# The end of a convolution-attention kernel in written order: the recurrence takes its PSUM banks from the loop's pools

## Chip, cores and metric

One core of a Trainium2 chip runs the whole program. The metric is the device time of one execution in microseconds, and the median of several executions is quoted. All data are float32.

## What is computed

```python
# layer 0: convolution attention over 4096 positions, 4 images, 128 channels
x = x + L0_conv_ref(gn(x), ...)
# layer 1, on tokens
t = to_tokens(x)
h = ln_t(t); q = h @ W
t = t + softmax(q @ q.T) @ h
# feed-forward part: a product, batch norm over all tokens, a recurrence over tokens
Wx = ln_t(t) @ W.T
Wx = (Wx - mean) * rsqrt(var + eps) * gamma + beta
def step(yt, wx_t):
    yt = sigmoid(wx_t + yt @ V.T)
    return yt, yt
t = t + scan(step, y0 = 0, Wx)
```

`mean` and `var` run over all 4 x 4096 tokens, so no step of the recurrence can start before the last product of the feed-forward part has been seen.

## The kernel before

For each of the four images `layer0` runs one attention and `layer1` the other; blocks of 512 tokens (`QB`, numbered `n`) are the unit. `layer1` works on a symmetric score matrix: a block of it serves its own tokens directly (`direct`) and, turned, those of another block (`reversed_products`). When all parts of a block's output have been added up in `oacc`, `finish` puts three small pieces of work on the queue `pending`, from which the loop takes one at a time between its products:

- `tokens` (L652 to L659, then `layernorm`, L297 to L301): transposes to tokens, denominators, residual, statistics of the normalisation on VectorE, the inverse square root on GpSimd (L143, L144), the normalised tokens on VectorE.
- `turn` (L672, L673): transposes back, a copy to SBUF on ScalarE; its `result` turns the tokens on VectorE (L273, into the tile `d`) and sends them to DRAM (`t2_d`, L277).
- `inputs` (L681 to L685): the feed-forward product, its statistics for the batch norm (`bn_st`), and a copy into `wxs`.

In the last image the blocks 1 and 0 come last. Block 0 takes its PSUM banks for this from `ps_s`, a pool of two tiles of two banks each that the scores use otherwise; the other blocks take theirs from `ps_m` (one tile of one bank). `ps_o` has three tiles of one bank. In all eight banks.

Then comes the end of `fast`: a comparison of all denominators with bounds (`ok`, L820 to L822), the batch norm's `gain` and `bias` (L845 to L850), and the recurrence. A chain of 32 tokens is one unit, and each chain begins 12 tokens earlier from zero, so there are 44 steps (k = 0 to 43); a step handles all chains at once, split into two halves by image (`halves`). For each half a step is: a preload of the bank with `gain * wx` on VectorE (`preload`, L864), a product with `V` added onto it on TensorE (L877), and the sigmoid with `bias` on ScalarE (L881), whose result is the operand of the next product of this half. The preload for step k + 2 stands behind step k in the code. Three banks in rotation for each half make six banks, six tiles of a pool of their own (`ps_r`). Before the first preload each bank is written once with a product (L841, six of 256 columns), since the recurrence's products add onto what is there. From step 15 on VectorE also adds a finished group of outputs to the tokens, one addition per step (L891), and four stores send the result out (L896). A check of the chains' overlap (`gap`, L900 to L904) and a branch on it close the program.

The order of instructions on each engine is set by a scheduler which works with a model of costs. Exceptions are stretches under `manual_schedule`, which stand as written, and single instructions marked by `keep_in_program_order`. Waits between engines are made from the tiles that instructions read and write.

Of the kernel before, what the change touches and what calls it, by code (L numbers as in the profile page):

```python
# [10 lines left out]
F32 = mybir.dt.float32  # L11
I32 = mybir.dt.int32
AF = mybir.ActivationFunctionType
ALU = mybir.AluOpType
AX = mybir.AxisListType
PSUM = bass.MemoryType.PSUM
DRAM = bass.MemoryType.DRAM

P = 128
B, C, N = 4, 128, 4096  # L20
# [3 lines left out]
NT = N // P  # L24
EPS_GN, EPS_LN, EPS_BN = 1e-5, 1e-5, 1e-5
# [4 lines left out]
QB = 512  # L30
# [6 lines left out]
G = N // L  # L37
GB = QB // L


DEN_LO, DEN_HI = 2.0**-60, 2.0**100
# [4 lines left out]
SQ, BQ, SK, BK, SG, BG, GAMMA, BETA = range(8)  # L46
# [124 lines left out]
def fast(  # L171
# [3 lines left out]
    nc = tc.nc  # L175
    keep_ctx = ExitStack()
    keep = keep_ctx.enter_context(tc.tile_pool(name="keep", bufs=1))
    bn_st = keep.tile([P, B * NB, 6], F32, name="bn_st")
# [6 lines left out]
    with ExitStack() as st:  # L185
# [2 lines left out]
        accp = st.enter_context(tc.tile_pool(name="accp", bufs=1))  # L188
        work = st.enter_context(tc.tile_pool(name="work", bufs=1))
        stat = st.enter_context(tc.tile_pool(name="stat", bufs=4))  # L190
        ps_s = st.enter_context(tc.tile_pool(name="ps_s", bufs=2, space=PSUM))
        ps_o = st.enter_context(tc.tile_pool(name="ps_o", bufs=3, space=PSUM))
        ps_m = st.enter_context(tc.tile_pool(name="ps_m", bufs=1, space=PSUM))

# [94 lines left out]
        def layernorm(src, dst):  # L291

            mv = stat.tile([P, NQ, 2], F32, tag="mv", name="mv")
            rstd = stat.tile([P, NQ], F32, tag="rstd", name="rstd")
            for j in range(NQ):
                s6 = stat.tile([P, 6], F32, tag="s6", name="s6")
                nc.vector.bn_stats(s6, src[j])  # L297
                nc.vector.bn_aggr(mv[:, j, :], s6)  # L298
            inv_sqrt(rstd, mv[:, :, 1], EPS_LN)
            for j in range(NQ):  # L300
                nc.vector.tensor_scalar(  # L301
                    dst[j], src[j], mv[:, j, 0:1], rstd[:, j : j + 1],
                    ALU.subtract, ALU.mult,
                )
# [238 lines left out]
        def layer1(b, h, qt):  # L543
# [50 lines left out]
            def direct():  # L594
                n, a, i, e, o = fifo.popleft()
                for half in range(2):
                    nc.tensor.matmul(  # L597
                        o, lhsT=h[:, NQ * a + 2 * i + half, :], rhs=e[:, half, :],
                        start=(a == order(n)[0] and i == 0 and half == 0),
                        stop=(a == order(n)[-1] and i == 1 and half == 1),  # L600
                    )
                if a == order(n)[-1] and i == 1:
                    part(n, o)
# [24 lines left out]
            def finish(n):  # L628
                cs = bass.ts(n, QB)
                rinv = stat.tile([P, NQ], F32, tag="rinv", name="rinv")  # L630
                t = work.tile([P, 4, NQ, 32], F32, tag="t", name="t1", bufs=2)
                if b == B - 1 and n == 0:

                    one, two = (ep.tile([P, 2, QB], F32, tag="e", name="last") for _ in range(2))
                    h2, t1 = (one[:, r, :].rearrange("q (j c) -> q j c", j=NQ) for r in range(2))
                    th = two[:, 0, :]

                    def bank():
                        return ps_s.tile([P, 2, QB], F32, tag="s", name="ml")[:, 0, :]
                else:  # L640
                    h2 = work.tile([P, NQ, C], F32, tag="h2", name="h2")
                    th = work.tile([P, QB], F32, tag="th", name="th")
                    t1 = work.tile([P, NQ, C], F32, tag="og", name="t1b")

                    def bank():
                        return ps_m.tile([P, QB], F32, tag="m", name="m1")
                nc.sync.dma_start(t, t_d[b, n])

                def tokens():
                    m = bank().rearrange("q (j c) -> q j c", j=NQ)  # L650
                    for j in range(NQ):
                        nc.tensor.transpose(m[:, j, :], oacc[:, n, bass.ts(j, P)], ident)  # L652
                    at = (B + b) * NT + n * NQ
                    den = den_all[:, at : at + NQ]
                    nc.vector.tensor_reduce(den, m, AX.X, ALU.add)
                    nc.vector.tensor_scalar(den, den, 1.0 / C, None, ALU.mult)
                    nc.vector.reciprocal(rinv, den)
                    for j in range(NQ):
                        nc.vector.scalar_tensor_tensor(  # L659
                            t1[:, j, :].rearrange("q (p i) -> q p i", p=4),  # L660
                            m[:, j, :].rearrange("q (p i) -> q p i", p=4), rinv[:, j : j + 1],
                            t[:, :, j, :], ALU.mult, ALU.add,
                        )
                    layernorm(quarters(t1), quarters(h2))

                def result():
                    turn_out(t1.rearrange("q j (p i) -> q j p i", p=4), t2_d[b, :, cs])

                def turn():
                    m = bank()  # L670
                    for j in range(NQ):
                        nc.tensor.transpose(m[:, bass.ts(j, P)], h2[:, j, :], ident)  # L672
                    nc.scalar.copy(  # L673
                        th.rearrange("c (p j k) -> c j p k", j=NQ, p=4),
                        m.rearrange("c (j p k) -> c j p k", j=NQ, p=4),
                    )
                    result()

                def inputs():
                    m = bank()  # L680
                    nc.tensor.matmul(m, lhsT=wt["f"], rhs=th, start=True, stop=True)  # L681
                    nc.vector.bn_stats(bn_st[:, b * NB + n, :], m)
                    m = m.rearrange("p (g i s) -> p i g s", i=L // 2, s=2)
                    if b == B - 1:
                        nc.vector.tensor_copy(wxs[:, :, b, bass.ts(n, GB), :], m)  # L685
                    else:
                        wx = work.tile([P, L // 2, GB, 2], F32, tag="wx", name="wx")
                        nc.vector.tensor_copy(wx, m)
                        nc.sync.dma_start(wxs_d[b, :, :, bass.ts(n, GB), :], wx)

                if b == B - 1 and n == 0:
                    pending.appendleft(tokens)
                    pending.extend([turn, inputs])
                elif b == B - 1 and n < 4:
                    pending.extend([tokens, turn, inputs])
                else:
                    pending.extend([tokens, nothing, nothing, nothing, turn, inputs])


            for n in [NB - 2, NB - 1] + list(range(NB - 3, -1, -1)):  # L700
                o = None
# [53 lines left out]
                        turned.append((clock + 4, n, a, t))  # L755
            while fifo:
                direct()
            pending.extend([reversed_products] * len(turned))

        def own_bank(_):  # L760
            return ps_m.tile([P, 512], F32, tag="m", name="mp")
# [53 lines left out]
        flush()  # L815


        tc.keep_in_program_order(nc.scalar.activation(first_y, shift, AF.Sigmoid))
        ok = big.tile([P, 2, 2 * B * NT], F32, tag="oacc", name="ok")
        nc.vector.tensor_scalar(ok[:, 0, :], den_all, DEN_LO, None, ALU.is_ge)  # L820
        nc.vector.tensor_scalar(ok[:, 1, :], den_all, DEN_HI, None, ALU.is_le)
        nc.vector.tensor_reduce(par_ok[:, 1:2], ok.rearrange("p a b -> p (a b)"), AX.X, ALU.min)  # L822


    with ExitStack() as st:
        scan = st.enter_context(tc.tile_pool(name="scan", bufs=1))
        ps_r = st.enter_context(tc.tile_pool(name="ps_r", bufs=1, space=PSUM))
        t2 = scan.tile([P, B, N], F32, name="t2s")
        for b in range(B):
            nc.sync.dma_start(t2[:, b, :], t2_d[b])  # L830
        y = scan.tile([P, L // 2, B, G, 2], F32, name="y")
        state = scan.tile([P, B, G + 1], F32, name="state")
        nc.gpsimd.memset(state[:, :, 0:1], 0.0)

        HB = B // 2
        banks = [[ps_r.tile([P, 512], F32, tag=f"r{s}{i}", name="ps_r") for i in range(3)] for s in range(2)]
        for s in range(2):
            for i in range(3):  # L840
                nc.tensor.matmul(  # L841
                    banks[s][i][:, : HB * G], lhsT=ident, rhs=wxs[:, 0, :HB, :, 0],
                    start=True, stop=True, skip_group_check=True,
                )
        nc.vector.bn_aggr(mv, bn_st.rearrange("p a b -> p (a b)"))  # L845
        inv_sqrt(gain, mv[:, 1:2], EPS_BN)
        nc.vector.tensor_mul(gain, gain, col(GAMMA))

        nc.vector.tensor_mul(bias, mv[:, 0:1], gain)
        nc.vector.tensor_sub(bias, col(BETA), bias)  # L850

        halves = [slice(s * HB, (s + 1) * HB) for s in range(2)]
        steps = list(range(L - W, L)) + list(range(L))

# [14 lines left out]
        for k, i in enumerate(steps):  # L869
# [15 lines left out]
            if k >= W:  # L885
                todo.extend((i - 3, b) for b in range(B) if i % 4 == 3)
                for j in range(len(todo) if i == L - 1 else min(1, len(todo))):
# [7 lines left out]
                    if i0 == L - 4:  # L895
                        nc.sync.dma_start(out[b], t2[:, b, :])  # L896


        gap = scan.tile([P, B, G - 1], F32, name="gap")
        nc.vector.tensor_sub(gap, state[:, :, 1:G], at(y, L - 1, slice(0, B))[:, :, : G - 1])  # L900
# [406 lines left out]
```

## Time and profile before

| | us |
|---|---|
| median of 3 runs | 3049.04 (3047.84 to 3049.8) |
| profiled execution | 3049.66 |
| its span, first to last instruction | 3047.8 |
| mean granted TensorE clock | 0.993 |
| TensorE busy (matmul) | 2990.5 |
| VectorE busy | 1678.8 |
| ScalarE busy | 1033.2 |
| GpSimd busy | 219.4 |

The page of the profile lists the busy times, a strip of 40 slices, the chain of work that ended last, and the costliest groups of instructions. Times in the timeline are counted from the start of the span. An instruction of TensorE shows as passes: a float32 product has two, each with a weight load (PEld) and a matmul (PE).

The last product of the attention loop ends near 2944 us. What follows, up to the end of the span, is the stretch that the change touches: from 2944 to 2963 the last two blocks and the batch norm, from 2963 to 3020.7 the recurrence, then the stores.

### The profile page before, as it was taken

How to read it: one execution, taken by the hardware profiler on the slowest of the kernel's cores; microseconds unless marked ns; L12 is line 12 of the kernel's file. 1: busy time of each engine (PE TensorE's matmuls, PEld its weight loads, DVE VectorE, ACT ScalarE, POOL GpSimd, SP SyncE). 2: the span in 40 equal slices, each digit the busy share in tenths (PEclk: the TensorE clock that was granted, in tenths of full speed). 3: DMA queues.
4: the chain of work that ended last, by engine and by line, in shares of the span. 5: the costliest groups of instructions: out<-in, count | busy, mean ns of one | idle time of the engine just before them, and what ended most of it. 6: DMA issues, size and time to landing. Idle time of an engine off the chain costs nothing.

```text
span 3047.8 us, 31523 instructions
## 1 busy us (share of the span) xinstructions
PE 2990.5 (98%) x10720; PEld 1370.7 (45%) x10720; DVE 1678.8 (55%) x3113; ACT 1033.2 (34%) x1150; POOL 219.4 (7%) x215
## 2 busy tenths in 40 slices
PE   8999999999999999999999999999999999999985
PEld 4444444444444444444444444444444444444442
DVE  6666654434666664443466665443456666333356
ACT  3444432222344432222244443222234443222224
POOL 0111100000011110000011011000001111000000
PEclk9999999999999999999999999999999999999998
DMA  1111143434111123343312114343422112544333
GB/s 42 39 55 56 51 115 87 96 88 101 44 56 56 44 86 97 91 101 85 89 46 56 39 49 117 85 99 88 99 59 56 42 49 88 145 100 101 97 117 153
DMA packets 247562, 241.09 MB, mean 79 GB/s; under 512 B 90080, under 2 KB 162272, under 8 KB 246368
## 3 DMA queue, kind: packets, MB, share of 16 engines
q1 hardware_dynamic: 247392, 238.98, 29.4%
q8 instruction: 88, 1.44, 0.2%
q14 instruction: 82, 0.67, 0.1%
HBM read 65.80 MB, written 56.62 MB: 40 GB/s over the span
## 4 chain that ended last, share of the span: by engine, by line
PE 93%; DVE 3%; SPq 2%; ACT 1%; DMA 0%; issue 0%; POOL 0%; DVEq 0%; ACTq 0%; POOLq 0%
PE o L468 28%; PE o L597 15%; PE ps L236 14%; PE ps L718 14%; PE ot L610 12%; SPq L752 2%; PE m L265 1%; PE m L681 1%; PE mp L430 1%; PE ps L570 1%; PE mp L366 1%; PE mq L562 1%; PE mp L415 1%; DVE t2s L891 1%; DVE ps_r L864 1%; PE m L672 1%
## 5 line engine op out<-in xcount | busy, mean ns | idle before, releaser
L468 PE MATMUL o<-e,nxt 64*128 64x512 f32 x4096 | 973.1, 589 | 0.0
L238 ACT ACTIVATE e<-ps 128x1024 f32<-128x1024 f32 x512 | 521.6, 1025 | 687.1 <-PE ps L236 649.7
L245 DVE TENSOR_TENSOR acc<-acc,e 128x1024 f32<-128x1024 f32 x448 | 547.7, 1223 | 230.7 <-ACT e L238 214.0
L468 PEld LDWEIGHTS o<-e,nxt 64*128 64x128 f32 x4096 | 403.3, 187 | 483.0 <-issue 474.2
L236 PE MATMUL ps<-nxt 64*128 64x512 f32 x2048 | 541.6, 595 | 1.3 <-ACT e L584 0.8
L597 PE MATMUL o<-e,h 128*128 128x512 f32 x1160 | 537.0, 592 | 0.0
L722 ACT ACTIVATE e<-ps,shift 128x1024 f32<-128x1024 f32 x258 | 287.4, 1114 | 646.3 <-PE ps L718 360.4
L718 PE MATMUL ps<-qt 128*128 128x512 f32 x1032 | 482.9, 594 | 2.7 <-ACT qt L563 2.7
L610 PE MATMUL ot<-tt,h 128*128 128x512 f32 x888 | 400.9, 593 | 0.0
L725 DVE STREAM_TRANSPOSE dd<-e 128x512 f32<-128x512 f32 x444 | 281.7, 683 | 137.1 <-ACT e L722 91.9
L597 PEld LDWEIGHTS o<-e,h 128*128 128x128 f32 x1160 | 218.8, 190 | 268.2 <-issue 268.0
L236 PEld LDWEIGHTS ps<-nxt 64*128 64x128 f32 x2048 | 197.9, 187 | 230.3 <-issue 148.6
L718 PEld LDWEIGHTS ps<-qt 128*128 128x128 f32 x1032 | 189.9, 190 | 219.3 <-issue 189.6
L610 PEld LDWEIGHTS ot<-tt,h 128*128 128x128 f32 x888 | 167.8, 190 | 210.2 <-issue 204.9
L619 DVE TENSOR_TENSOR oacc<-oacc,ot 128x512 f32<-128x512 f32 x87 | 59.8, 687 | 288.2 <-PE ot L610 288.2
L143 POOL TENSOR_SCALAR rstd<-mv 128x4 f32<-128x4 f32 x64 | 14.6, 228 | 2371.6 <-DVE mv L298 2371.6
L524 DVE SCALAR_TENSOR_TENSOR t<-yt,rinv,t 128x128 f32<-128x128 f32 x128 | 36.5, 347 | 78.1 <-DMA yt<-turn_d 78.1
L485 POOL TENSOR_SCALAR xb<-xb,bpc 128x512 f32<-128x512 f32 x32 | 59.7, 1866 | 250.6 <-DMA xb<-in_x_dram 244.9
L535 POOL TENSOR_SCALAR h<-h 128x512 f32<-128x512 f32 x32 | 72.4, 2262 | 63.8 <-DVE d L273 61.7
L580 ACT ACTIVATE e<-ps,shift 128x512 f32<-128x512 f32 x32 | 22.0, 687 | 143.5 <-PE ps L576 118.5
L144 POOL TENSOR_TENSOR rstd<-rstd,mhalf 128x4 f32<-128x4 f32 x64 | 66.4, 1038 | 5.3
L621 DVE COPY oacc<-ot 128x512 f32<-128x512 f32 x24 | 16.6, 692 | 87.2 <-PE ot L610 87.1
(156 smaller groups left out, 1613.5 us busy)
## 6 DMA issues: line engine op xcount, KB each, us to landing
tt<-dd SPq DMA_DIRECT2D x1776, 64.0 KB, 2.0
turn_d<-d SPq DMA_DIRECT2D x384, 64.0 KB, 1.8
xb<-in_x_dram SPq DMA_DIRECT2D x32, 256.0 KB, 3.3
t<-turn_d SPq DMA_DIRECT2D x32, 256.0 KB, 2.7
yt<-turn_d SPq DMA_DIRECT2D x32, 256.0 KB, 2.7
t_d<-t SPq DMA_DIRECT2D x32, 256.0 KB, 2.0
qt<-turn_d SPq DMA_DIRECT2D x32, 256.0 KB, 2.8
t<-t_d SPq DMA_DIRECT2D x32, 256.0 KB, 2.9
```

Of the source, the lines that this page charges most:

```text
L144: nc.gpsimd.tensor_tensor(dst, dst, mhalf[:, :n], ALU.pow)
L236: nc.tensor.matmul(ps[:, h, :], lhsT=lhsT, rhs=rhs, start=True, stop=True)
L238: nc.scalar.activation(e, ps, AF.Exp, scale=scale)
L245: nc.vector.tensor_tensor(acc, acc, e, ALU.add)
L468: nc.tensor.matmul(o[r], lhsT=v[rs, p + h * PAIRS, :], rhs=e[rs, h, :], start=(p == 0 and h == 0), stop=(p == PAIRS - 1 and h == 1),)
L535: nc.gpsimd.tensor_scalar(hn, hn, 1.0, None, ALU.add)
L597: nc.tensor.matmul(o, lhsT=h[:, NQ * a + 2 * i + half, :], rhs=e[:, half, :], start=(a == order(n)[0] and i == 0 and half == 0), stop=(a = ...
L610: nc.tensor.matmul(ot, lhsT=h[:, NQ * n + j, :], rhs=t[:, :, j, :, :].rearrange("q p k j -> q k p j"), start=(j == 0), stop=(j == NQ - 1),)
L718: nc.tensor.matmul(ps[:, half, :], lhsT=qt[:, bass.ts(at, P)], rhs=qt[:, bass.ts(n, QB)], start=True, stop=True,)
L722: nc.scalar.activation(e, ps, AF.Exp, bias=shift)
L725: nc.vector.transpose(d.rearrange("q f b k j -> q k b f j")[:, 2 * i + half], e[:, half, :].rearrange("q (b f j) -> q b f j", b=NQ, f=NQ),)
L752: nc.sync.dma_start(t[bass.ts(f, 32), p], d[bass.ts(p, 32), f])
```

## The change

It does five things.

1. The three PSUM pools live until the end of `fast`, and the recurrence's six banks come from them. The function `take_banks`, called in `tokens` of the last image's block 0 behind its transposes, takes both tiles of `ps_s` (each tile gives one bank for half 0 and one for half 1), one tile of `ps_o` and the tile of `ps_m`. It marks the six banks with products of 256 columns from `oacc` and adds four products of 512 columns into one of them. The pool `ps_r` and the marks at L841 are gone.
2. Block 0 of the last image takes its banks from `ps_o` instead of `ps_s`.
3. From behind the last loop product of the last image everything stands as written (`manual_schedule`).
4. In this stretch the order is another: `bn_aggr` and the gain come ahead of the copy of block 0 into `wxs`; the comparison of the denominators stands behind the recurrence; block 1's `tokens` come with `nothing` behind them.
5. `layernorm` writes each aggregate one statistic later.

```diff
-        ps_s = st.enter_context(tc.tile_pool(name="ps_s", bufs=2, space=PSUM))
-        ps_o = st.enter_context(tc.tile_pool(name="ps_o", bufs=3, space=PSUM))
-        ps_m = st.enter_context(tc.tile_pool(name="ps_m", bufs=1, space=PSUM))
+        ps_s = keep_ctx.enter_context(tc.tile_pool(name="ps_s", bufs=2, space=PSUM))
+        ps_o = keep_ctx.enter_context(tc.tile_pool(name="ps_o", bufs=3, space=PSUM))
+        ps_m = keep_ctx.enter_context(tc.tile_pool(name="ps_m", bufs=1, space=PSUM))
...
+            sums: deque = deque()
             for j in range(NQ):
                 s6 = stat.tile([P, 6], F32, tag="s6", name="s6")
                 nc.vector.bn_stats(s6, src[j])
-                nc.vector.bn_aggr(mv[:, j, :], s6)
+                sums.append((mv[:, j, :], s6))
+                if j > 0:
+                    nc.vector.bn_aggr(*sums.popleft())
+            nc.vector.bn_aggr(*sums.popleft())
...
                     def bank():
-                        return ps_s.tile([P, 2, QB], F32, tag="s", name="ml")[:, 0, :]
+                        return ps_o.tile([P, QB], F32, tag="o", name="ml")
...
                         nc.tensor.transpose(m[:, j, :], oacc[:, n, bass.ts(j, P)], ident)
+                    if b == B - 1 and n == 0:
+                        take_banks(oacc[:, 1, :])
...
-                    if b == B - 1:
+                    if b == B - 1 and n == 0:
+                        last_inputs.append(m)
+                    elif b == B - 1:
                         nc.vector.tensor_copy(wxs[:, :, b, bass.ts(n, GB), :], m)
...
+                elif b == B - 1 and n == 1:
+                    pending.extend([tokens, nothing, turn, inputs])
...
             while fifo:
                 direct()
+            if b == B - 1:
+
+                keep_ctx.enter_context(tc.manual_schedule())
             pending.extend([reversed_products] * len(turned))
+        HB = B // 2
+        banks = [[None] * 3 for _ in range(2)]
+        last_inputs = []
+
+        def take_banks(some):
+            def mark(m, cols):
+                nc.tensor.matmul(
+                    m[:, :cols], lhsT=ident, rhs=some[:, :cols], start=True, stop=True,
+                    skip_group_check=True,
+                )
+
+            for i in (1, 2):
+                pair = ps_s.tile([P, 2, QB], F32, tag="s", name="ps_r")
+                for r in range(2):
+                    banks[r][i] = pair[:, r, :]
+            banks[0][0] = ps_o.tile([P, QB], F32, tag="o", name="ps_r")
+            banks[1][0] = ps_m.tile([P, QB], F32, tag="m", name="ps_r")
+            for r in range(2):
+                for i in range(3):
+                    mark(banks[r][i], HB * G)
+            for _ in range(4):
+                mark(banks[0][0], QB)
...
-        tc.keep_in_program_order(nc.scalar.activation(first_y, shift, AF.Sigmoid))
-        ok = big.tile([P, 2, 2 * B * NT], F32, tag="oacc", name="ok")
-        nc.vector.tensor_scalar(ok[:, 0, :], den_all, DEN_LO, None, ALU.is_ge)
-        nc.vector.tensor_scalar(ok[:, 1, :], den_all, DEN_HI, None, ALU.is_le)
-        nc.vector.tensor_reduce(par_ok[:, 1:2], ok.rearrange("p a b -> p (a b)"), AX.X, ALU.min)
+        nc.scalar.activation(first_y, shift, AF.Sigmoid)
+        nc.vector.bn_aggr(mv, bn_st.rearrange("p a b -> p (a b)"))
+        inv_sqrt(gain, mv[:, 1:2], EPS_BN)
+        nc.vector.tensor_copy(wxs[:, :, B - 1, :GB, :], last_inputs[0])
+        nc.vector.tensor_mul(gain, gain, col(GAMMA))
...
-        ps_r = st.enter_context(tc.tile_pool(name="ps_r", bufs=1, space=PSUM))
...
-        banks = [[ps_r.tile([P, 512], F32, tag=f"r{s}{i}", name="ps_r") for i in range(3)] for s in range(2)]
-        for s in range(2):
-            for i in range(3):
-                nc.tensor.matmul(
-                    banks[s][i][:, : HB * G], lhsT=ident, rhs=wxs[:, 0, :HB, :, 0],
-                    start=True, stop=True, skip_group_check=True,
-                )
-        nc.vector.bn_aggr(mv, bn_st.rearrange("p a b -> p (a b)"))
-        inv_sqrt(gain, mv[:, 1:2], EPS_BN)
-        nc.vector.tensor_mul(gain, gain, col(GAMMA))
...
+        ok = scan.tile([P, 2, 2 * B * NT], F32, name="ok")
+        nc.vector.tensor_scalar(ok[:, 0, :], den_all, DEN_LO, None, ALU.is_ge)
+        nc.vector.tensor_scalar(ok[:, 1, :], den_all, DEN_HI, None, ALU.is_le)
+        nc.vector.tensor_reduce(par_ok[:, 1:2], ok.rearrange("p a b -> p (a b)"), AX.X, ALU.min)
```

## The prediction

> **What bounds the kernel now.** The change touches only what follows the last loop product, so I read the chain of waits over the last 150 us first, then the timeline there, then the table of stretches with the granted clock. The page's chain gives PE 93%: up to 2944 us the loops are TensorE's own work, and nothing there is edited. From 2944 on the chain hops between engines. Columns: start us, us, what.
>
> ```profile
> 2949.29 0.59 DVE wxs L685
> 2951.13 0.60 DVE d L273
> 2952.19 1.05 POOL rstd L144
> 2953.66 1.26 PE ml L672 x4
> 2954.95 0.59 ACT last L673
> 2955.59 2.09 PE ml L681 x2
> 2957.70 0.70 DVE bn_st L682
> 2958.40 0.60 DVE wxs L685
> 2959.13 4.82 PE ps_r L841 x12
> ...
> 2965.73 0.49 ACT y L881
> 2966.27 0.73 PE ps_r L877 x2
> 2967.03 0.50 ACT y L881
> 2967.57 0.73 PE ps_r L877 x2
> ...
> 3017.86 0.59 DVE t2s L891
> 3018.45 0.79 DVE ps_r L864 x2
> 3019.23 3.60 DVE t2s L891 x6
> ```
>
> Three things to see. The six bank marks (L841) stand on the chain for 4.82 us. In the recurrence one half costs 0.76 us from the start of its product to the start of its sigmoid (2966.27 to 2967.03) and 0.54 us from there to its next product: 1.30 us a step. Near the end VectorE sets the pace: 0.79 for two preloads and 0.59 for one addition, 1.38 us. How two halves fit into 1.30 us shows the timeline (start, us, engine, line, what; in brackets the idle time before):
>
> ```profile
> 2966.27 0.30 PEld L877 LDWEIGHTS ps_r<-y,w 128*128 128x128 f32 x2 [0.53 <-ACT y L881]
> 2966.74 0.30 PEld L877 LDWEIGHTS ps_r<-y,w 128*128 128x128 f32 x2 [0.18 <-ACT y L881]
> 2967.03 0.97 ACT L881 ACTIVATE y<-ps_r,bias 128x256 f32<-128x256 f32 x2 [0.34 <-PE ps_r L877]
> ```
>
> The second half's product starts at 2966.74, 0.29 us before the first half's sigmoid of the same step. The halves overlap by half a step. The clock (stretch, length, busy time of PE, PEld, DVE, ACT, POOL, then PEclk):
>
> ```profile
> 2944.00:2948.60 4.60, 2.74 (x11) 1.22 (x10) 3.71 (x13) 0.59 (x1) 1.08 (x2) 1.00 0.23 57
> 2948.60:2953.60 5.00, 0.00 (x0) 0.00 (x0) 4.39 (x16) 0.00 (x0) 1.27 (x2) 0.58 0.11 28
> 2953.60:2956.00 2.40, 1.66 (x5) 1.14 (x6) 0.78 (x4) 1.03 (x2) 0.00 (x0) 0.50 0.20 51
> 2961.00:2963.50 2.50, 2.50 (x8) 2.00 (x7) 2.01 (x7) 1.12 (x2) 0.00 (x0) 0.58 0.98 419
> 2963.50:2966.00 2.50, 2.38 (x10) 1.29 (x9) 1.90 (x4) 1.22 (x3) 0.00 (x0) 1.00 1.00 423
> ```
>
> The clock falls to half at about 2949.5, after TensorE thinned out, and returns at about 2963.1 under the marks, just before the recurrence.
>
> **What the skill says.** "TensorE: Matmul & The Clock Gate", Part 1: half clock after an idle window of 3413 ns, full after a busy one, in free-running windows. The trace agrees: 2949.5 to 2963.1 is 13.6 us, four windows. "PSUM — Partial Sum Buffer", on bank collisions: engines have to be kept apart by bank, and different banks may be used at once. The recurrence before agrees: six banks in six tiles, and TensorE writes one while ScalarE reads another.
>
> **Part 1: the banks.** Before, six tiles of one bank. After, steps k with k mod 3 = 1 or 2 take both halves' banks from one two-bank tile of ps_s; only k mod 3 = 0 has separate tiles (ps_o, ps_m). Waits are made per tile, not per bank. In the changed program's instruction list the second half's product of such a step waits for the first half's sigmoid of the same step, where before it waited for its own half's sigmoid of the step before. The hardware doesn't need that wait, but it is executed.
>
> Step by step, from first-half product h0 and second-half product h1: in a pair step h1 starts 1.30 after h0 (0.76 + 0.54). The next step's h0 needs no further wait and follows h1 at once; its sigmoid follows h1's by 0.45 us (two sigmoids in 0.94 us at 3012.84, where products already run back to back). So h1 to next h1 is 0.76 + 0.45 + 0.54 = 1.75 us. Into k mod 3 = 0, h1 waits for its own half: 1.30. From there h0 of the next step starts at 1.75 and its h1 at 1.75 + 1.30 = 3.05. Three steps: 3.05 + 1.75 = 4.80 us, 1.60 a step against 1.30 to 1.37 now. VectorE fits below that: per three steps two preload pairs that now wait for each other (0.49 + 0.06 + 0.39, about 0.95 each), one of 0.79 and three additions of 0.59 make 4.46 us; so the additions no longer set the pace.
>
> Products run for k = 1 to 43. From the first to the second h1: 3.05; 13 rounds of 4.80: 62.4; the last two steps to the end of the last sigmoid: 3.05 + 0.76 + 0.49 = 4.30. Sum 69.75 us. Before: from 2963.56 to 3020.66, 57.1. **Loss 12.65 us.**
>
> **Part 2: from 2944 to the first product.** The instruction list shows what moves; one end for each:
> - L820 goes behind the recurrence, and the fourth L659 comes ahead of L682. The two early marks beside the L672 transposes (256 columns at 0.43 us each: L570 has 0.86 for four passes, and a product has two) and one between those transposes delay the n = 1 product by some 0.2 us: L682 at 2948.8 instead of 2948.6, statistics of n = 0 at 2950.0 (before 2950.06).
> - The transpose into d (L273, 0.60) leaves the gap ahead of the last aggregate: rstd is done about 0.6 us sooner, h2 ready at 2953.75 instead of 2954.4.
> - The other three marks and the four extra products stand on TensorE ahead of the h2 transposes. The first of them waits for the n = 1 copy (its bank), 2950.0. At full clock 3 x 0.43 + 4 x 0.86 = 4.7 us: to 2954.75, 1.0 us past h2. Then four transposes 0.6 us (1.26 at half clock before), copy 0.59, product 1.15 to the statistics (2.1 before): L682 at 2957.2 instead of 2957.70. At half clock they would last to 2959.4; I take full, since the early marks raise TensorE's work in the window before 2949.5.
> - The aggregate goes ahead of the wxs copy, which then lies beside GpSimd: gain ready at 2960.0 instead of 2960.93, bias at 2960.55 instead of 2961.76. L841 is gone from behind it.
> - The first product waits for both preloads of its tile, 2960.5 + 0.49 + 0.06 + 0.49 + 0.05: 2961.6 instead of 2963.56. **Gain 1.9 us.**
> - Moved DMAs: the four t2_d stores now leave SP after h2, near 2954.5; with 1.77 us to issue four and 1.8 to land they end near 2958, before the sigmoid that waits for them at 2960.6. The t2s loads still follow the n = 0 product. The memset stands behind the gain on GpSimd and nobody waits for it before step 12. All nothing.
>
> **Part 3: the clock at the start of the recurrence.** TensorE is now idle from 2957.0 to 2961.6, 4.6 us, longer than a window: the clock falls to half before the recurrence. There a product costs 0.43 more and a step about 2.3 us. Until one busy window has passed (1.7 to 6.8 us, half a window taken plus one, 5.1) each us loses 1 - 1.6/2.3 = 0.3: **loss 1.5 us**, bounds 0 and, if the clock never returns, 43 x 0.7 = 30.
>
> **Part 4: the end.** VectorE is no longer behind: the first output store leaves 0.5 us before the last sigmoid ends, not 0.39 after it. The stores still take 22 us. **Gain 0.9 us.** The ok operations (0.26 + 0.26 + 0.69) lie beside these stores, as the gap check (done at 3026) does: nothing. The new order of aggregates in layernorm leaves VectorE's order in the loops as it was: nothing.
>
> **Sum:** 12.65 - 1.9 + 1.5 - 0.9 = +11.35 us. The profiled execution took 3049.66 for a span of 3047.8; the median of the runs is 3049.04, 0.6 less. So 3061.0 for that execution and 3060.4 for a median.
>
> **Rivals.**
> - A, as worked out: 3057 to 3064. Chance 0.62.
> - B, the clock drops again and again. Products fill 6 x 0.43 of 4.80 us, 54%. A window of 55% (7.2 to 10.6 us, the tail of the warming products) kept full clock, one of 35% (2946.1 to 2949.5) lost it; two pair steps alone fill 49%. Each drop costs 1 to 2 us: 3064 to 3077. Chance 0.18.
> - C, it never returns. At half clock the products fill 5.16 of 6.9 us, 75%; the window to 2959.7 with some 51% did not lift it, the full one to 2963.1 did. 3077 to 3091. Chance 0.1.
> - D, the chained halves cost less than half of what I work out, since another overlap makes up for it: 3050 to 3056. Chance 0.06.
> - E, faster: the front of the recurrence alone decides, without marks, ok work and transpose. That is right if the halves still overlap: then -1.9 - 0.9 = 3046.2. It decides as soon as a step stays under 1.36 us on average (57.1 / 43 = 1.33 now, and parts 2 to 4 leave 1.3 over 43 steps). For it speaks that the banks are as distinct as before, against it the wait in the program. Chance 0.04.
>
> The forecast is that of A, 3060.4. The range 3056 to 3077 holds A and B. A measurement of this kernel can tell about 0.2% (6 us) from no change: slower 0.93, same 0.04, faster 0.03.
>
> **What would show it.** In the changed trace: second-half weights loading 0.54 us after the first half's sigmoid begins, not before it; sigmoids in a rhythm of 1.75, 1.75, 1.30 us; VectorE with idle time in the recurrence; the first recurrence product near 2961.6; half clock there for one or two windows; the L783 products up to 2954.8. Wrong would be a step of 1.3 us in the recurrence, half clock in its middle, or a first product after 2964.

## The result, and the profile after

| | before | after |
|---|---|---|
| median, 6 runs each (us) | 3047.96 (3047.32 to 3049.80) | 3060.57 (3058.69 to 3061.04) |
| profiled execution | 3049.66 | 3060.72 |
| its span | 3047.8 | 3059.0 |
| front: last addition into `oacc` to first product of the recurrence | 19.46 | 17.58 |
| recurrence: first product to end of last sigmoid | 57.1 | 72.95 |
| behind the last sigmoid | 27.2 | 25.6 |

The ratio is 1.004, with a 95% interval of 1.0029 to 1.0051: the changed kernel is 12.6 us slower. The lower three rows split this difference. The front starts with VectorE's last addition into `oacc` (at 2944.10 before, at 2942.90 after). The span grew by 11.2 us. The front gives -1.9, the recurrence +15.85, the end -1.6, and what lies ahead of the front -1.2: the profiled run of before began with one more window of half clock, at 17 to 21 us, in code that the change does not touch. (Of the eleven profiled executions here, the four with such an extra window near their start have that addition at 2943.97 to 2944.21, the other seven at 2942.54 to 2942.97.)

The chain of waits of the changed kernel (start us, us, what) runs through the front into the recurrence:

```profile
2948.90 5.00 PE ps_r L783 x14
2953.89 0.45 PE ml L678 x4
...
2955.00 1.14 PE ml L687 x2
2956.17 0.71 DVE bn_st L688
...
2959.48 0.41 DVE ps_r L888
2959.92 0.50 DVE ps_r L888
...
2960.51 1.21 PE ps_r L901 x2
...
2964.93 3.89 PE ps_r L901 x8
```

The marks (L783) are still on the chain and take 5.00 us against 4.82 before, but they now stand ahead of the last feed-forward product and run at full clock. Behind them the four transposes take 0.45 us and the product 1.14, against 1.26 and 2.09. (For the transposes the clock is not the main reason, as experiment 5 shows.) Two preloads (L888) stand one behind the other ahead of the first product, as the wait on the pair tile demands. Eight passes in 3.89 us are 0.49 each; the clock is at half there, as the stretches further down show.

ScalarE's timeline in the recurrence of the changed kernel (start, us, engine, line, what; in brackets the idle time before), where the clock is full again:

```profile
2970.13 0.94 ACT L905 ACTIVATE y<-ps_r,bias 128x256 f32<-128x256 f32 x2 [0.81 <-PE ps_r L901]
2971.89 0.94 ACT L905 ACTIVATE y<-ps_r,bias 128x256 f32<-128x256 f32 x2 [0.81 <-PE ps_r L901]
2973.18 0.94 ACT L905 ACTIVATE y<-ps_r,bias 128x256 f32<-128x256 f32 x2 [0.35 <-PE ps_r L901]
```

Each line is two sigmoids: that of the second half of one step and, right behind it, that of the first half of the next. The starts are 1.76 and 1.29 us apart; the next, at 2974.93 in the chain, is 1.75 further. The long distances show 0.81 us of idle ScalarE, the short one 0.35.

TensorE's side, some steps later (the same kind of view):

```profile
2985.49 0.75 PEld L901 LDWEIGHTS ps_r<-y,w 128*128 128x128 f32 x4 [1.00 <-ACT y L905]
2986.78 0.30 PEld L901 LDWEIGHTS ps_r<-y,w 128*128 128x128 f32 x2 [0.55 <-ACT y L905]
2987.24 0.30 PEld L901 LDWEIGHTS ps_r<-y,w 128*128 128x128 f32 x2 [0.15 <-ACT y L905]
2988.53 0.75 PEld L901 LDWEIGHTS ps_r<-y,w 128*128 128x128 f32 x4 [1.00 <-ACT y L905]
```

A line with four weight loads is one second-half product and the first-half product of the next step, back to back, behind 1.00 us without a load. The cause of that idle time is ScalarE's y. The load at 2988.53 comes right behind the second of the two sigmoids that run from 2987.55 to 2988.49; its own operand is the result of the first, so it has waited for the sigmoid of the *other* half. Where a step has separate tiles, its second half (2986.78) loads after a gap of 0.55, and the first half of the next step 0.46 us behind it (2987.24), each behind its own sigmoid.

The stretches of the changed kernel around the start of the recurrence, cut where the granted clock changes (stretch, length, busy time of PE, PEld, DVE, ACT, POOL, then PEclk and DMA):

```profile
2955.57:2958.98 3.41, 0.56 (x2) 0.00 (x0) 2.31 (x4) 0.88 (x2) 0.86 (x3) 1.00 0.55 131
2958.98:2962.39 3.41, 1.31 (x3) 0.62 (x3) 2.96 (x9) 1.61 (x3) 0.00 (x0) 0.50 0.95 408
2962.39:2965.81 3.42, 2.84 (x6) 1.84 (x7) 0.97 (x2) 0.97 (x2) 0.00 (x0) 0.50 1.03 441
2965.81:2969.22 3.41, 2.99 (x7) 1.38 (x6) 1.84 (x4) 1.84 (x4) 0.00 (x0) 0.50 1.01 432
2969.22:2972.63 3.41, 2.55 (x9) 1.55 (x10) 1.20 (x3) 1.79 (x5) 0.00 (x0) 1.00 0.99 423
```

After a window with 0.56 us of products the clock was at half for three windows, from 2958.98 to 2969.22. The middle one of the three, with TensorE busy for 2.84 of 3.42 us, did not bring the full clock back; the last one, with 2.99, did.

### The profile page after: what moved, and what is told of

It reads as the page before. It is cut to its first block, busy times and chain, and to the rows that moved or that the text cites. A ratio compares the mean times of both kernels' runs of the same rounds, so it can differ in the third digit from the quotient of the medians.

```text
span 3059.0 us, 31491 instructions
## 1 busy us (share of the span) xinstructions
PE 2991.4 (98%) x10728; PEld 1372.9 (45%) x10728; DVE 1680.7 (55%) x3113; ACT 1031.5 (34%) x1150; POOL 218.5 (7%) x215
## 4 chain that ended last, share of the span: by engine, by line
PE 93%; DVE 2%; SPq 2%; ACT 2%; issue 0%; DMA 0%; POOL 0%; DVEq 0%; POOLq 0%
PE o L472 28%; PE o L601 15%; PE ps L236 14%; PE ps L728 14%; PE ot L614 12%; SPq L762 2%; PE ps_r L901 1%; PE m L265 1%; ACT y L905 1%; PE m L687 1%; PE mp L434 1%; PE ps L574 1%; PE mq L566 1%; PE mp L370 1%; PE mp L419 1%; PE m L678 1%
## 5 line engine op out<-in xcount | busy, mean ns | idle before, releaser
L901 PE MATMUL ps_r<-y,w 128*128 128x256 f32 x168 | 52.8, 437 | 22.9 <-ACT y L905 16.4
L144 POOL TENSOR_TENSOR rstd<-rstd,mhalf 128x4 f32<-128x4 f32 x64 | 66.4, 1037 | 5.3
```

Source lines behind the costliest of these rows:

```text
L144: nc.gpsimd.tensor_tensor(dst, dst, mhalf[:, :n], ALU.pow)
L901: nc.tensor.matmul(bank(k, s), lhsT=wt["vt"], rhs=before, start=False, stop=True, skip_group_check=True,)
```

## The experiments

Two theories stood at the outset. The *tile theory*: the wait that the pair tile makes between the two halves costs some 13 us in the recurrence. The *clock theory*: the new front, with its marks, its extra products and its gap, lets the clock fall, and the recurrence is slow for that. They differ in what a kernel does that has the new front without pairs, or the pairs without the new front.

**1. The changed kernel, six separate tiles (`r1_split`).** The pools are the same; two tiles of `ps_s` give one bank each, and the last tile of `ps_o` is taken once block 0 has been copied out of it.

```diff
             for i in (1, 2):
-                pair = ps_s.tile([P, 2, QB], F32, tag="s", name="ps_r")
-                for r in range(2):
-                    banks[r][i] = pair[:, r, :]
-            banks[0][0] = ps_o.tile([P, QB], F32, tag="o", name="ps_r")
-            banks[1][0] = ps_m.tile([P, QB], F32, tag="m", name="ps_r")
-            for r in range(2):
-                for i in range(3):
-                    mark(banks[r][i], HB * G)
+                banks[0][i] = ps_s.tile([P, 2, QB], F32, tag="s", name="ps_r")[:, 0, :]
+                banks[1][i] = ps_o.tile([P, QB], F32, tag="o", name="ps_r")
+            banks[0][0] = ps_m.tile([P, QB], F32, tag="m", name="ps_r")
+            for r, i in ((0, 1), (1, 1), (0, 2), (1, 2), (0, 0)):
+                mark(banks[r][i], HB * G)
...
+        banks[1][0] = ps_o.tile([P, QB], F32, tag="o", name="ps_r")
+        nc.tensor.matmul(
+            banks[1][0][:, : HB * G], lhsT=ident, rhs=bc.rearrange("p a b -> p (a b)")[:, : HB * G],
+            start=True, stop=True, skip_group_check=True,
+        )
```

> The changed kernel with six separate tiles for the six banks (one bank each of the two ps_s tiles, two of ps_o, ps_m, and the last one taken from ps_o behind the copy of block 0); marks and the four extra products stay. Theory of the tile's wait: the halves overlap again, a step takes 1.30 us at full clock and 1.73 at half, the recurrence from first product to last sigmoid 57 to 60 us instead of 72.95; the whole 3046 to 3049. Rival, the half clock at the start and the written order are the cost: the rhythm of 1.75, 1.75, 1.30 stays, the recurrence takes over 68 us, the whole 3058 to 3061.

Measured: 3046.39 us (3045.41 to 3047.04), against 3047.91 for the kernel before on the same chip; ratio 0.9994 (0.9985 to 1.0003). The recurrence went from 72.95 to 58.2 us. The timeline of this kernel's recurrence:

```profile
2972.51 0.30 PEld L903 LDWEIGHTS ps_r<-y,w 128*128 128x128 f32 x2 [0.25 <-ACT y L907]
2972.73 1.03 ACT L907 ACTIVATE y<-ps_r,bias 128x256 f32<-128x256 f32 x2 [0.27 <-PE ps_r L903]
2973.26 0.30 PEld L903 LDWEIGHTS ps_r<-y,w 128*128 128x128 f32 x2 [0.45 <-ACT y L907]
2973.81 0.30 PEld L903 LDWEIGHTS ps_r<-y,w 128*128 128x128 f32 x2 [0.25 <-ACT y L907]
2974.02 0.48 ACT L907 ACTIVATE y<-ps_r,bias 128x256 f32<-128x256 f32 x1 [0.26 <-PE ps_r L903]
```

The weights at 2972.51 are those of the first half's product. They load 0.22 us before the second half's sigmoid of the step before starts (2972.73). The second half's own weights follow at 2973.26, when that sigmoid has ended; the first half's sigmoid of their step only begins then (2973.27). No half waits for the other any more, and the next pair of sigmoids follows after 1.29 us. Besides the tiles only the order of the six marks changed, and the place and source of one of them. With nearly the same front, and with half clock at the start of the recurrence here too (until 2964.71), the slow recurrence is gone, which the clock theory does not allow. The whole is not clearly different from the kernel before.

**2. Pairs along the other axis (`r2_by_half`).** One line: a tile of `ps_s` now holds two steps' banks of *one* half, so that the halves are free of each other again, and a half is tied to itself.

```diff
                 for r in range(2):
-                    banks[r][i] = pair[:, r, :]
+                    banks[i - 1][r + 1] = pair[:, r, :]
```

> The changed kernel with the two-bank tiles dealt out the other way: each ps_s tile holds two steps' banks of one half. Theory of the tile's wait: the products of the two halves no longer wait for each other, only preloads and products of neighbouring steps of one half do; two steps of 1.30 and one of 1.4 at first, and of up to 2.0 once VectorE's additions stand between; the recurrence 62 to 66 us, the whole 3050 to 3055. Rival, two banks next to each other cost as such, whichever waits there are: the recurrence stays at 70 to 73 us, the whole at 3058 to 3062.

Measured: 3053.25 us (3051.61 to 3055.0), ratio 1.0016 (1.0009 to 1.0023); recurrence about 64 us. Its ScalarE timeline:

```profile
2986.87 0.94 ACT L905 ACTIVATE y<-ps_r,bias 128x256 f32<-128x256 f32 x2 [0.36 <-PE ps_r L901]
2988.90 0.94 ACT L905 ACTIVATE y<-ps_r,bias 128x256 f32<-128x256 f32 x2 [1.09 <-PE ps_r L901]
2990.20 0.94 ACT L905 ACTIVATE y<-ps_r,bias 128x256 f32<-128x256 f32 x2 [0.36 <-PE ps_r L901]
2991.49 0.94 ACT L905 ACTIVATE y<-ps_r,bias 128x256 f32<-128x256 f32 x2 [0.36 <-PE ps_r L901]
```

Now two steps of three take 1.30 us and one 2.03. Earlier in this recurrence, before VectorE's additions begin (2983.70), the long step takes 1.42. What is late is in the view of waits of this kernel from 2980 on (who waits for whom: us in total, times, longest):

```profile
PE ps_r L901 <- DVE ps_r L888: 7.3, 9, 0.9
```

TensorE waits for VectorE's preloads, nine times. It fits that the preloads of two steps now share a tile, so that the earlier step's product also waits for the later step's preload, at a time when VectorE has its additions to do; which wait it is was not followed further. 57.1 + 7.3 = 64.4 lies near the 64 us, but the sum is rough: this recurrence also has half clock until 2966.2. How much a pair costs depends on which two users share it, not only on there being one.

**3. The kernel before, with pairs alone (`r3_before_pairs`).** The counterpart: nothing of the change but the shape of the tiles, in the old pool `ps_r`.

```diff
-        banks = [[ps_r.tile([P, 512], F32, tag=f"r{s}{i}", name="ps_r") for i in range(3)] for s in range(2)]
+        pairs = [ps_r.tile([P, 2, 512], F32, tag=f"p{i}", name="ps_r") for i in range(2)]
+        alone = [ps_r.tile([P, 512], F32, tag=f"r{s}", name="ps_r") for s in range(2)]
+        banks = [[alone[s], pairs[0][:, s, :], pairs[1][:, s, :]] for s in range(2)]
```

> The kernel before with nothing changed but the tiles of the recurrence's banks: steps with k mod 3 = 1 and 2 have both halves in one two-bank tile. The marks stay ahead of the recurrence, so the clock is full there. Theory of the tile's wait: the rhythm of 1.75, 1.75, 1.30 us, the recurrence 69.5 to 70.5 us instead of 57.1, the end about 1 us closer behind it, the whole 11 to 12.5 us above the kernel before, 3059 to 3061. Rival, it takes the pools of the loop or the written order: no change, 3047 to 3049.

Measured: 3069.54 us in the median of four runs, ratio 1.0071 (1.0054 to 1.0088), and the four runs fall apart: 3061.04, 3067.66, 3071.42 and 3071.59. The first is the profiled one; its mean clock is 0.995, that of the others 0.989 to 0.991. Its recurrence takes 70.1 us at full clock, and its ScalarE timeline has the rhythm of the changed kernel (1.75, 1.30, 1.75):

```profile
2989.09 0.94 ACT L883 ACTIVATE y<-ps_r,bias 128x256 f32<-128x256 f32 x2 [0.81 <-PE ps_r L879]
2990.84 0.94 ACT L883 ACTIVATE y<-ps_r,bias 128x256 f32<-128x256 f32 x2 [0.81 <-PE ps_r L879]
2992.14 0.95 ACT L883 ACTIVATE y<-ps_r,bias 128x256 f32<-128x256 f32 x2 [0.35 <-PE ps_r L879]
2993.89 0.94 ACT L883 ACTIVATE y<-ps_r,bias 128x256 f32<-128x256 f32 x2 [0.81 <-PE ps_r L879]
```

So the tiles alone, without any of the new front, bring 13 us: 70.1 against 57.1. The median is outside of what was expected, by 8.5 us, and the mean clock says where to look. That needed a profile of one of the long runs.

**4. The same kernel, three more executions (`r7_pairs_again`, `r8_pairs_third`, `r9_pairs_fourth`).**

> The kernel before with tiles of two banks once more, for a trace of a run of about 3070 us: three of its four runs took 3067.7 to 3071.6 at a mean clock of 0.989 to 0.991, one 3061.0 at 0.995. If the clock falls inside the recurrence, the table of stretches shows half clock there for several windows and steps of about 2.6 us, and the recurrence lasts some 80 us; if the profile is again of a run of about 3061, steps stay at 1.75, 1.75, 1.30 and it lasts 70 us.

> The kernel before with tiles of two banks, a third time, for the trace of a run above 3066 us. If the clock falls inside the recurrence: half clock there, steps of about 2.6 us, the recurrence over 75 us. Otherwise 70 us and 3061.

> The same kernel a fourth time, with the same two outcomes: above 3066 us with half clock inside the recurrence, or 3061 with full clock.

Measured: 3061.9, 3061.51 and 3070.89 us; the clocks 0.994, 0.994 and 0.990. The third is one of the long ones. First the stretches of the short run `r7_pairs_again`, then those of the long run `r9_pairs_fourth`, again window by window:

```profile
2957.88:2961.30 3.42, 3.30 (x8) 2.69 (x9) 1.69 (x5) 0.52 (x2) 0.81 (x2) 0.50 0.78 316
2961.30:2964.71 3.41, 1.89 (x8) 0.96 (x6) 2.17 (x5) 1.07 (x3) 0.00 (x0) 1.00 1.04 440
2964.71:2968.13 3.42, 2.64 (x9) 1.64 (x10) 1.29 (x3) 1.79 (x5) 0.00 (x0) 1.00 0.97 417
```

```profile
2960.95:2964.36 3.41, 3.41 (x9) 2.65 (x9) 1.22 (x5) 1.12 (x2) 0.81 (x2) 0.50 0.97 413
2964.36:2967.77 3.41, 1.82 (x7) 0.94 (x7) 1.77 (x5) 0.49 (x1) 0.00 (x0) 1.00 1.02 430
2967.77:2971.18 3.41, 2.83 (x8) 1.64 (x6) 0.97 (x2) 1.25 (x3) 0.00 (x0) 0.50 0.99 423
...
2984.84:2988.25 3.41, 2.88 (x7) 1.33 (x5) 1.85 (x4) 1.95 (x4) 0.00 (x0) 0.50 0.00 0
2988.25:2991.66 3.41, 2.67 (x10) 1.65 (x10) 1.34 (x3) 1.80 (x4) 0.00 (x0) 1.00 0.00 0
```

Both get the full clock back under the marks. The first window at full clock holds the tail of the marks, a gap, and the first products. In the short run TensorE is busy for 1.89 of its 3.41 us (55%), and the clock stays; in the long run for 1.82 (53%), and it falls. Then the paced recurrence keeps TensorE busy for 2.83 or 2.84 of each window, which did not lift the clock five times in a row; it took six windows until one with 2.88 did. At half clock three steps take 7.10 us (sigmoids at 2971.76, 2978.86 and 2985.95), against 4.80. Over 20.5 us that is 20.5 x (1 - 4.80 / 7.10) = 6.6 us. The recurrence also starts 2.6 us later (2966.1 against 2963.5), 1.2 of them from ahead of block 1's inverse square root (L144 at 2944.18 and 2943.00) and 1.4 from the front, where this run was at half clock sooner. 6.6 + 2.6 = 9.2, against 9.0 for the two spans (3069.2 and 3060.2). The other three long runs were not profiled. Their clocks are like this one's; that they have the same cause is likely and not shown.

**5. Without the extra products (`r4_no_extra`).** The changed kernel less these two lines:

```diff
-            for _ in range(4):
-                mark(banks[0][0], QB)
```

> The changed kernel without the four extra products of 512 columns; the six marks stay. Theory: the transposes of the last block start when its tokens are ready, 1.1 us sooner; if the clock holds, the whole is 1.1 us shorter; if it falls in the gap, the transposes take 0.6 and the product 0.9 us longer and nothing is won: 3059.0 to 3061.0, the recurrence unchanged at 71 to 73.5. Rival, the extra products are what holds TensorE up and costs the time: 4 us shorter, 3056.5.

Measured: 3059.42 us, ratio 1.0042 (1.0025 to 1.0059); four runs, three within 3059.33 to 3059.49 and one of 3065.31 with a clock of 0.991, not profiled. The chain of waits of this kernel, by the side of that of the changed kernel shown above:

```profile
2951.14 0.36 DVE last L305
...
2951.54 1.11 PE ml L678 x4
...
2953.32 1.33 PE ml L687 x2
2954.67 0.71 DVE bn_st L688
...
2959.01 1.21 PE ps_r L899 x2
```

Its stretches, cut where the granted clock could change (every 3.41 us):

```profile
2947.30:2950.71 3.41, 1.56 (x6) 1.06 (x6) 2.37 (x10) 0.00 (x0) 0.87 (x2) 1.00 0.00 0
2950.71:2954.12 3.41, 1.90 (x6) 0.85 (x6) 1.73 (x5) 1.42 (x2) 0.40 (x1) 1.00 0.09 21
2954.12:2957.53 3.41, 0.51 (x1) 0.00 (x0) 2.36 (x4) 0.65 (x2) 0.86 (x3) 0.50 0.46 106
```

The four transposes take 1.11 us here and 0.45 in the changed kernel, but that is not the clock, which is full until 2954.12. Each transpose needs its own quarter of the normalised tokens, and VectorE (L305) finishes one about every 0.26 us from 2951.14 on; in the changed kernel the extra products hold the transposes back until all quarters are there, and they run in one go. (`r6_all` below has the same 1.11 us, at full clock throughout.) The clock falls only inside the product, which takes 1.33 us instead of 1.14. So the extra products do hold the clock, but that is worth only 0.19 us ahead of the statistics. Against it they stand in front of the transposes. Counted from the inverse square root of block 1 (L144, at 2942.63 here and 2942.92 there), the transposes end 1.4 us sooner without them, and the first product of the recurrence comes 1.2 us sooner. What they buy is less than what they cost, by 1.2 us.

**6. Products in the gap (`r5_fill`).** The changed kernel with four products of 512 columns behind the last feed-forward product, where TensorE has nothing to do while VectorE and GpSimd work out gain and bias:

```diff
+        for _ in range(4):
+            nc.tensor.matmul(
+                banks[0][0], lhsT=ident, rhs=bc.rearrange("p a b -> p (a b)"),
+                start=True, stop=True, skip_group_check=True,
+            )
```

> The changed kernel with four more products of 512 columns (from the constant bc, into a bank that is still free) behind the last feed-forward product, where TensorE was idle for 4.4 us; nothing else. Theory: the clock is full when the recurrence starts, its first two steps take 1.75 instead of 2.65, it lasts 70 to 70.5 us instead of 72.95, the whole 2.5 to 3 us shorter, 3057.5 to 3058.5, with single runs up to 10 us longer where the clock falls inside the recurrence, as in the kernel before with tiles of two banks. Rival, the time lost at the start is the longer way to the first product and not the clock: no change, 3060 to 3061.

Measured: 3058.71 us (3058.2 to 3060.03), ratio 1.0033 (1.002 to 1.0047). Its stretches:

```profile
2957.00:2961.50 4.50, 3.63 (x9) 1.33 (x7) 3.65 (x9) 1.31 (x4) 0.87 (x3) 1.00 0.68 215
2961.50:2965.00 3.50, 2.26 (x8) 1.33 (x9) 2.47 (x6) 1.78 (x4) 0.00 (x0) 1.00 1.02 435
```

The clock is full throughout. The recurrence takes 70.2 us, 2.8 less than in the changed kernel: the price of half clock at its start. The four products delay nothing: from the end of the last feed-forward product to the first product of the recurrence it is 4.38 us here (2957.20 to 2961.58) and in the changed kernel (2956.13 to 2960.51).

**7. All together (`r6_all`).** Six tiles as in 1, the four products as in 6, and two extra products in place of four.

```diff
-            for _ in range(4):
+            for _ in range(2):
                 mark(banks[0][0], QB)
```

> Six separate tiles, two extra products instead of four ahead of the last block's transposes, and four behind the last feed-forward product. Theory: first product of the recurrence 1 us sooner than in the changed kernel, full clock there, steps of 1.30 us, the recurrence 56.5 to 57.5 us; the whole 3043.5 to 3045.5, about 3 us under the kernel before and 2 us under six tiles alone. Rival, the front doesn't get shorter because the products stand in the way: 3046 to 3048.

Measured: 3043.92 us (3042.55 to 3045.61, 21 runs), against 3049.02 (26 runs) for the kernel before on the same chip; ratio 0.9984 (0.9978 to 0.9991). It is faster than both kernels. Its chain of waits:

```profile
2951.73 1.11 PE ml L678 x4
...
2953.50 1.14 PE ml L687 x2
...
2958.82 0.73 PE ps_r L907 x2
2959.58 0.49 ACT y L911
2960.07 0.04 issue
2960.12 0.73 PE ps_r L907 x2
2960.87 0.49 ACT y L911
```

The first product of the recurrence takes 0.73 us, not 1.21, and from there a step takes 1.30. From the oacc addition to that product it is 16.04 us (before: 19.46), and the recurrence takes 56.7 (before: 57.1).

## Why the prediction was right

The forecast was 3060.4 us, slower; the median is 3060.57. That the totals agree within 0.2 us is in part luck: the forecast stood on a median before of 3049.04, and that of the six runs is 3047.96, so the change forecast was +11.35 us and the change measured is +12.6. By its own steps:

- **Part 1, the banks (12.65 us):** right, in mechanism and in size. The rhythm of 1.75, 1.75 and 1.30 us is in the trace to 0.01 us. At full clock throughout, the recurrence took 70.1 to 70.2 us (`r3_before_pairs`, `r5_fill`), where 69.75 was worked out. Taking only the pairs away removed 14.75 us (`r1_split`), of which a part is clock, since half clock ended sooner there. With the pairs and without at full clock it is 70.2 against 56.7 (`r5_fill`, `r6_all`), and adding only the pairs to the kernel before brought 13 (`r3_before_pairs`).
- **A small thing in part 1 was off.** That VectorE "fits below" is right for most of the recurrence; the last four rounds of three steps took 4.91 to 4.92 us instead of 4.80, 0.48 us in all, while VectorE was busy for 92% of the time. Whether VectorE is the cause was not tried.
- **Part 2, the front (gain 1.9):** right, 1.88. The marks ended at 2953.9, the last statistics began at 2956.17, the first product at 2960.5; each is 0.8 to 1.1 us ahead of the forecast time, which is the 1.2 us that this run was ahead from the beginning, less 0.1 to 0.4. One reading in it was wrong without harm to the sum: the 1.26 us of the four transposes before were put down to half clock, but at full clock they took 1.11 (`r4_no_extra`, `r6_all`), at the pace of VectorE's quarters. They are short in the changed kernel only because the extra products make them late, which cost the path 1.2 us.
- **Part 3, the clock (loss 1.5):** right in mechanism, too small. The term was 5.1 us at half clock; it was 8.7 us of the recurrence, since the window with 2.84 us of products did not count as a busy one. Twice two steps took 4.42 and 4.45 us (from the first product at 2960.51 to a product at 2964.93, and from there to 2969.38) for what takes 3.05 at full clock: 2.8 us lost, and 2.8 by the difference to `r5_fill`. The "half a window taken plus one" should have been two windows and a half.
- **Part 4, the end (gain 0.9):** right. The first store leaves 0.54 us ahead of the last sigmoid's end (3032.89 and 3033.43), where it was 0.39 behind. From the first store to the end of the span it took another 0.7 less (26.1 against 26.8), which was not foreseen.

The terms add up: 12.65 + 2.8 + 0.48 is 15.9, against 15.85 for the recurrence. The total for the profiled execution (3061.0 forecast, 3060.72 measured) came out nearly exact in part because the 1.3 us missing in part 3 and the 0.5 in part 1 were made good by 0.7 at the end and by the 1.2 us ahead of the front, which were not in the sum.

Of the rivals, B (the clock falls inside the recurrence) did not show in the times of the six runs of the changed kernel, of which one was profiled. It is no idle one: the kernel before with the same pairs fell into it in the one long run that was profiled. C (it never returns) had the right observation, that the paced recurrence does not lift the clock, but in that run it came back after six windows. D and E are out: the wait is real and nothing makes up for it. The shares that the prediction gives under B and C for three windows of the kernel before (55, 35 and 51%) are not the busy shares of the profile, which has 60% (2.04 of 3.41 us), 51% (1.72 of 3.40) and 57% (1.95 of 3.42). So its 54% for the paced recurrence can't be set beside the busy times quoted here.

On the Trainium skill: "PSUM — Partial Sum Buffer" has it, on bank collisions, that engines have to be kept apart by bank. `r1_split` shows that nothing more is needed in this recurrence, since with a tile for each bank ScalarE reads one while TensorE writes another, at 1.29 us a step. "TensorE: Matmul & The Clock Gate", Part 1, has the clock come back after one busy window of some 3.4 us. The lengths agree (in the traces here every stretch at half clock within the work is a multiple of 3.41 us); what counts as busy is stricter than a TensorE that is seldom idle, as 2.84 of 3.42 us did not do.

## What to carry to other kernels

Waits follow the tile, so two banks in one tile tie everything that uses them: give each of two chains that are to overlap its own tile, and when tiles are re-used from another pool, look at who shares them with whom before counting what the pool saved. In a chain of small products, read the wait of a late instruction and ask whether it is for its own operand or only for its neighbour's. Products that keep the clock belong into TensorE's idle time (`r5_fill`), not ahead of the work that the path waits for (`r4_no_extra`).

## What was not expected of the hardware

The granted clock sits near an edge in this recurrence, and the profile's busy time of TensorE shows it on one side only. At half clock windows with up to 2.84 of 3.41 us did not regain the full clock, and windows with 2.88 and more did, in all the traces here. At full clock the busy time does not sort the windows: 1.82 (`r9_pairs_fourth`) and 1.90 (`r4_no_extra`) lost it, while 1.89 (`r7_pairs_again`) and even 1.56 (`r4_no_extra`) kept it. The busy times contain modelled ends, so these are marks of this kernel and no thresholds, and what decides at full clock stays open. But such a fall made up 6.6 of the 9.0 us by which the one long run that was profiled exceeds a short one. Of seven runs of the kernel before with pairs, three took 3061 to 3062 and four 3068 to 3072.
